# A four-layer vision network on one core: who goes first while the last image is sampled, and which engine makes the feed-forward's casts after the scan

## The chip, the cores and the metric

The kernel runs on one core of one Trainium2 chip. The core has a matrix engine (TensorE, in the profile PE, with PEld for its weight loads), a vector engine (VectorE, DVE), a scalar engine (ScalarE, ACT), a general engine (GpSimd, POOL) and a queue for transfers (SyncE, SP). Each engine works through its own list of instructions in order; semaphores tie the lists together. The metric is the time of one execution on the device, in microseconds (us), lower is better.

## The reference, cut to what matters

Four images of 96 channels and 64x64 pixels pass through four layers, each added to its input:

```python
# layer 0: group norm, depthwise conv, selective scan in four directions, gate, projection
x = x + _L0_conv_ref(_gn(x), ...)
# layer 1: group norm, deformable 3x3 convolution (9 taps, bilinear sampling, mask)
x = x + _L1_conv_ref(_gn(x), ...)
t = _to_tokens(x)                        # 4096 tokens of 96
# layer 2: Fourier mixing, then a feed-forward in quantized arithmetic
t = t + _L2_attn_ref(_ln_t(t), ...)
t = t + _L2_ffn_ref(_ln_t(t), ...)
# layer 3: linear attention, then the same feed-forward with other weights
t = t + _L3_attn_ref(_ln_t(t), ...)
t = t + _L3_ffn_ref(_ln_t(t), ...)
```

The feed-forward (`_qlinear` twice, with a ReLU between) rounds each factor to a float of 5 exponent and 2 mantissa bits and each sum to 5 and 10 bits. In the kernel these are casts to an fp8 and an fp16 type: 96 to 384 to 96 values per token.

## The kernel before, in words

**Three kinds of work, two streams and a scan.** Layer 0's selective scan (`Layer0.scan`) is one long loop of 1536 units; it sets the pace of the program until about 7904 us. Everything else is written as generators that hand out small steps: an instruction or a few, with a cost for each engine that the planner books. Two streams of such steps exist (`layers23`, at the end of the file). `ends()` is stream 0: it prepares layer 0's inputs and then takes image 0, 1, 2 and 3 through layers 2 and 3 (`Layers23.image`), one after the other. `middle()` is stream 1: for each image it finishes layer 0 (`Layer0.behind`) and does layer 1 (`Layer1.image`). An image may enter layers 2 and 3 only when its layer 1 is through (`while b not in self.net.sampled`), and only when the image before it has left.

**The planner.** `Clock` keeps, at build time, an end of planned work for each engine. A step is issued if the engines that it needs are not booked too far ahead (`AHEAD`) and its inputs are planned to be ready; otherwise the stream is passed over. `go()` asks both streams for a step, in a fixed order: `reversed(streams)`, so stream 1 has the first choice. What is issued is recorded, and `in_program_order` fixes that order on each engine. `pipe` does the same inside a stream, among the chains of one stage. The order of the instructions is thus settled when the program is built; the chip only follows it. The scan's `goes` steps take part until it ends; then the scan's PSUM banks are given back, `net.own_banks` is set (five banks for stream 0, three for stream 1), and `alone()` runs the two streams until both are over.

**Sampling an image** (`Layer1.sample`, helper `taps`). An image has 32 blocks of 128 pixels with 9 taps each, taken three at a time: 96 triples. For a triple GpSimd issues three indirect transfers (L1301), each fetching for 128 pixels the four corners of a tap from a table in DRAM; they land in a buffer `g`, of which there are six. VectorE multiplies by the four weights (L1310). Once `own_banks` is set, VectorE also adds the corners (L1314, L1315), so that TensorE needs 3 transposes (L1327) instead of 12; ScalarE copies them to `st` (L1335), which frees `g`. After six triples TensorE applies the convolution's weights (L1343), VectorE adds bias and input (L1348), and SyncE stores the piece (L1350).

**Layers 2 and 3 of an image.** SyncE loads the image, `t` (L1679). `Fourier.run` normalises, multiplies by DFT matrices (L1421 the 64x64 ones) and adds to `t` (L1508). `Ffn.run` normalises into `tl` (L1525, in `normed`; the trace calls it `fl`) and works in 8 chunks of 512 tokens, up to four at once: a cast to `xq` (L1567; two buffers), three matmuls (L1572) with copies to `h16` (L1573; two buffers), bias and ReLU in three pieces (on VectorE, L1578, once `own_banks` is set, else on ScalarE, L1582), a cast to `h8` (L1585; two buffers), three matmuls (L1589), a copy to `o16` (L1591; two buffers), the bias (L1594 or L1596) and the residual add (L1598). Both casts are GpSimd's:

```python
nc.gpsimd.tensor_copy(xq, tl[:, cs], saturate=False)      # L1567
nc.gpsimd.tensor_copy(h8, h16, saturate=False)            # L1585
```

`LinearAttention.run` comes between the two feed-forwards; it begins with a memset on GpSimd (L1618) and ends with adds to `t` (L1654). At the end SyncE stores `t` (L1686).

Of the kernel before, what the change touches and what calls it, by code (L numbers as in the profile page):

```python
# [19 lines left out]
B, C, H, W = 4, 96, 64, 64  # L20
# [152 lines left out]
class Step:  # L173
# [5 lines left out]
    def __init__(self, work, wait=0.0, holds=0, new=False, takes="", frees=""):  # L179
        self.work, self.wait, self.holds, self.new = work, wait, holds, new  # L180
        self.takes, self.frees = takes.split(), frees.split()


def cost(pe=0.0, dve=0.0, act=0.0, pool=0.0, **more):
    return Step((pe, dve, act, pool), **more)


def wait(us=0.0, **more):

    return Step((0.0,) * 4, us, **more)  # L190
# [155 lines left out]
class Net:  # L346
# [3 lines left out]
    def __init__(self, ctx, tc, ins):  # L350
        self.tc, self.nc, self.ins = tc, tc.nc, ins
        nc = self.nc
        self.const = ctx.enter_context(tc.tile_pool(name="const", bufs=1))
        self.dram = ctx.enter_context(tc.tile_pool(name="scratch", bufs=1, space=DRAM))
        self.psum = ctx.enter_context(tc.tile_pool(name="mm", bufs=3, space=PSUM))
        for name in ("vecs", "ident", "cen96", "grp3", "add4"):
            setattr(self, name, self.load(name, self.const))

        self.to_row = {}
        for n in (C, DI):  # L360
            t = self.to_row[n] = self.const.tile([128, 65], F32, name=f"to_row{n}")
            nc.vector.memset(t, 0.0)
            nc.vector.memset(t[:, 1:2], 1.0 / n)
        self.eps = self.const.tile([128, 1], F32, name="eps")
        nc.vector.memset(self.eps, 1e-5)
        self.one = self.const.tile([128, 1], F32, name="one")
        nc.vector.memset(self.one, 1.0)
        self.minus_one = self.const.tile([128, 1], F32, name="minus_one")
        nc.vector.memset(self.minus_one, -1.0)
        self.exp_and_log()  # L370

        self.sampled = set()
        self.clock, self.known, self.streams, self.stream = Clock(), {}, [], None

        self.own_banks = None
# [740 lines left out]
class Layer1:  # L1116
# [23 lines left out]
    def image(self, b):  # L1140
        tc = self.net.tc
        with tc.tile_pool(name=f"l1i{b}", bufs=1, side="right") as ix:
            idx = ix.tile([128, 288], U32, name=f"idx{b}", tag="idx")
            wt = ix.tile([128, 288, 4], F32, name=f"wt{b}", tag="wt")
            yield from self.before(b, idx, wt)
            yield from self.sample(b, idx, wt)
        self.net.sampled.add(b)

# [208 lines left out]
class Fourier:  # L1357
# [77 lines left out]
    def run(self, b, t):  # L1435

        net = self.net
        tc, nc = net.tc, net.nc
        with tc.tile_pool(name=f"l2b{b}", bufs=1) as big:
            tl = big.tile([C + 1, L], F32, name=f"tl{b}", tag="tl")  # L1440
            nc.gpsimd.memset(tl[C:], 1.0)
            with tc.tile_pool(name=f"l2n{b}", bufs=2) as pool:
                yield from normed(net, t, tl, f"2_{b}", pool)
            tv = tl.rearrange("c (n1 n2) -> c n1 n2", n2=64)
            with tc.tile_pool(name=f"l2s{b}", bufs=2) as pool:
                for g in range(2):
                    yield from self.half(f"{b}_{g}", g, tv, t, pool, pool)
# [83 lines left out]
class Ffn:  # L1531
# [23 lines left out]
    def run(self, b, t):  # L1555
        net, n = self.net, self.n
        tc, nc = net.tc, net.nc
        with tc.tile_pool(name=f"fb{n}_{b}", bufs=1) as big, tc.tile_pool(name=f"fs{n}_{b}", bufs=2) as pool:
            tl = big.tile([C, L], F32, name=f"fl{n}_{b}", tag="tl")
            yield from normed(net, t, tl, f"f{n}_{b}", pool)  # L1560

            def chunk(j):
                yield wait(takes="xq")
                cs = slice(j * CH, (j + 1) * CH)
                key = f"f{n}_{b}_{j}"
                xq = pool.tile([C, CH], F8, name=f"xq{key}", tag="xq")
                nc.gpsimd.tensor_copy(xq, tl[:, cs], saturate=False)  # L1567
                yield cost(pool=0.8, new=True, takes="h16")
                h16 = pool.tile([128, 3, CH], F16, name=f"h16{key}", tag="h16")
                for g in range(3):  # L1570
                    ph = net.mm(f"ph{key}_{g}")
                    nc.tensor.matmul(ph, lhsT=self.w1[:, 128 * g : 128 * g + 128], rhs=xq, start=True, stop=True)  # L1572
                    nc.scalar.copy(h16[:, g], ph)  # L1573
                yield cost(pe=1.3, act=1.8, frees="xq")
                if net.own_banks:
                    for g in range(3):
                        bias = self.bias[:, g : g + 1]
                        nc.vector.tensor_scalar(h16[:, g], h16[:, g], bias, 0.0, ALU.add, ALU.max)  # L1578
                    yield cost(dve=1.5, takes="h8")
                else:  # L1580
                    for g in range(3):
                        nc.scalar.activation(h16[:, g], h16[:, g], AF.Relu, bias=self.bias[:, g : g + 1])  # L1582
                    yield cost(act=2.1, takes="h8")
                h8 = pool.tile([128, 3, CH], F8, name=f"h8{key}", tag="h8")
                nc.gpsimd.tensor_copy(h8, h16, saturate=False)  # L1585
                yield cost(pool=1.5, new=True, takes="o16", frees="h16")
                po = net.mm(f"po{key}")
                for g in range(3):
                    nc.tensor.matmul(po, lhsT=self.w2[:, g, :], rhs=h8[:, g], start=(g == 0), stop=(g == 2))  # L1589
                o16 = pool.tile([C, CH], F16, name=f"o16{key}", tag="o16")  # L1590
                nc.scalar.copy(o16, po[:C])  # L1591
                if net.own_banks:
                    yield cost(pe=1.3, act=0.6, frees="h8")
                    nc.vector.tensor_scalar_add(o16, o16, self.bias[:C, 3:4])  # L1594
                else:
                    nc.scalar.activation(o16, o16, AF.Identity, bias=self.bias[:C, 3:4])  # L1596
                    yield cost(pe=1.3, act=1.3, frees="h8")
                nc.vector.tensor_add(t[:, cs], t[:, cs], o16)  # L1598
                yield cost(dve=1.0, frees="o16")

            yield from pipe(self.net, (chunk(j) for j in range(NCH)), 4, xq=2, h16=2, h8=2, o16=2)


# [93 lines left out]
def layers23(net, x2, out):  # L1697

    with ExitStack() as ctx:
        l0 = Layer0(ctx, net, net.x1)
        l1 = Layer1(ctx, net, net.x1, x2)

        def ends():
            yield from l0.before(0)
            l23 = Layers23(ctx, net, x2, out)
            yield from l23.prepare()
            yield from l0.before(1)  # L1710
            yield from l0.before(2)
            yield from l0.before(3)
            for b in range(B):
                yield from l23.image(b)

        def middle():
            yield from l1.cleared()
            for b in range(B):
                yield from l0.behind(b)
                yield from l1.image(b)  # L1720

        streams = net.streams = [Stream(net, ends()), Stream(net, middle())]
        clock = net.clock

        def go():

            return any([stream.step() for stream in reversed(streams)])

        def alone():

            if clock.own is None:
                clock.own = max(clock.ends)
            if not go():
                clock.own += 0.5

        for goes in l0.scan():
            if not goes:
                alone()
                continue
            if clock.own is not None:  # L1740
                clock.due = max(clock.due, clock.own + PACE)
                clock.idle = max(clock.idle, clock.due)
                clock.own = None
            while go():
                pass
        l0.banks.close()
        net.own_banks = ctx.enter_context(net.tc.tile_pool(name="own", bufs=5, space=PSUM))
        while not all(stream.over for stream in streams):
            alone()
        net.in_program_order()  # L1750
# [24 lines left out]
```

## Time and profile before

| what | value |
|---|---|
| median of 4 runs | 9101.74 us (9082.23 to 9113.54) |
| the profiled execution's own time | 9094.06 us |
| its span, first to last instruction | 9092.3 us |
| busy over the span | PE 72%, DVE 77%, POOL 70%, ACT 46% |
| last unit of the scan | 7904 us |
| image 3 sampled (L1310) | 8080 to 8532 us |
| image 2 in layers 2 and 3 (L1679 to L1686) | 7563 to 8626 us |
| image 3 in layers 2 and 3 | 8633 to 9084 us |

The page of the profile gives shares over the whole span, and most of the span is the scan. For a change that begins after the scan one has to ask for stretches: busy time in a window, groups of instructions in a window, and the order of single instructions on one engine. In a row of a group, "x96" is the count, then follow busy time, mean duration in ns of one, the engine's idle time just before these instructions, and what ended most of it. A releaser "issue" means that the engine waited for nothing that the profile shows.

### The profile page before, as it was taken

The numbers are of one execution on the slowest core, as the hardware profiler recorded it, in microseconds if no ns is written. First come the engines' busy times: TensorE is split into PE (matmuls) and PEld (weight loads), VectorE is DVE, ScalarE is ACT, GpSimd is POOL, SyncE is SP. The second block draws the span as 40 slices with busy tenths as digits, with TensorE's granted clock in tenths as the row PEclk, the third lists the DMA queues.
The fourth block names the chain that finished last, engine by engine and source line by source line (L and its number), as shares of the span: only waits on it lengthen the run. The fifth ranks groups of instructions, "written<-read, shape, count | busy, mean of one in ns | idle before, by whom it ended". The sixth has DMA issues, their size and how long they took to land.

```text
span 9092.3 us, 93188 instructions
## 1 busy us (share of the span) xinstructions
PE 6577.2 (72%) x31951; PEld 2981.8 (33%) x31960; DVE 6972.6 (77%) x4932; ACT 4183.6 (46%) x5798; POOL 6382.7 (70%) x4755
## 2 busy tenths in 40 slices
PE   6664977697766668777667777777777677874687
PEld 2111311132222234211224554223554332462374
DVE  0367878887788889888789898988999998636514
ACT  4564667565544435556443334554333444321223
POOL 0486679766788989788799895775898966538501
PEclk8675977798777779877778888878888887886788
DMA  1466787777777788787778878677888776644210
GB/s 51 125 185 167 189 203 223 195 192 191 192 209 207 205 205 221 194 211 208 201 205 203 224 205 193 171 172 188 214 212 213 190 176 171 156 129 138 76 54 12
DMA packets 775967, 1608.21 MB, mean 177 GB/s; under 512 B 247809, under 2 KB 339357, under 8 KB 773382
## 3 DMA queue, kind: packets, MB, share of 16 engines
q10 hardware_dynamic: 244224, 843.17, 37.0%
q1 hardware_dynamic: 457542, 532.51, 21.9%
q0 software_dynamic: 73728, 226.57, 9.4%
q8 instruction: 255, 4.18, 0.2%
q14 instruction: 218, 1.79, 0.1%
HBM read 1345.62 MB, written 256.29 MB: 176 GB/s over the span
## 4 chain that ended last, share of the span: by engine, by line
PE 33%; DVE 20%; DMA 15%; POOL 13%; issue 10%; ACT 6%; SPq 2%; ACTq 1%; another core or an unknown queue 0%; DVEq 0%; POOLq 0%
DVE hh L961 9%; POOL hh L970 6%; DVE db L953 5%; PE pc L692 5%; PE py L989 3%; PE ps L1327 3%; PE f L1421 3%; DMA du<-du 3%; PE db L939 3%; POOL g L1301 2%; PE pd L1343 2%; DVE g L1310 1%; DMA da<-de 1%; DMA m<-in_dft 1%; POOL lw L781 1%
## 5 line engine op out<-in xcount | busy, mean ns | idle before, releaser
L970 POOL TENSOR_TENSOR hh<-hh,bc 128x1024 f32<-128x1024 f32 x1536 | 3655.8, 2383 | 347.4 <-DVE hh L961 235.6
L961 DVE TENSOR_TENSOR_SCAN hh<-da,st,db 128x1024 f32<-128x1024 f32 x1152 | 2700.7, 2344 | 176.9 <-PE py L989 50.3
L953 DVE TENSOR_TENSOR db<-db,bc 128x1024 f32<-128x1024 f32 x1536 | 1864.5, 1214 | 510.9 <-PE db L939 495.2
L933 ACT ACTIVATE da<-da,w_al 128x1024 f32<-128x1024 f32 x1536 | 1740.1, 1147 | 847.7 <-DMA da<-de 395.3
L939 PE MATMUL db<-du,rep 96*128 96x512 bf16 x3072 | 1088.8, 443 | 816.5 <-DVE hh L961 725.1
L1301 POOL DMA_INDIRECT g<-table,idx x1152 | 1339.1, 1162 | 369.9 <-issue 233.9
L989 PE MATMUL py<-hh,w_fold 128*32 128x512 f32 x6144 | 1075.7, 741 | 87.2 <-POOL hh L970 64.3
L1327 PE MATMUL ps<-w_ident,g 128*96 128x128 f32 x3744 | 637.6, 333 | 517.1 <-issue 294.6
L961 DVE TENSOR_TENSOR_SCAN hh<-da,db 128x1024 f32<-128x1024 f32 x384 | 876.7, 2283 | 55.8 <-PE py L989 19.8
L939 PEld LDWEIGHTS <-rep 96*128 96x128 bf16 x3072 | 278.9, 106 | 1781.9 <-issue 1135.9
L1310 DVE TENSOR_TENSOR g<-g,wt 128x1152 f32<-128x1152 f32 x384 | 724.6, 1889 | 107.2 <-DMA g<-table,idx 96.9
L1327 PEld LDWEIGHTS ps<-w_ident,g 128*96 128x96 f32 x3744 | 517.9, 155 | 792.3 <-issue 417.4
L1335 ACT COPY st<-ps 96x384 f32<-96x384 f32 x384 | 181.9, 476 | 1256.7 <-PE ps L1327 954.8
L968 POOL COPY st<-hh 128x1 f32<-128x1 f32 x1152 | 303.6, 264 | 509.9 <-DVE hh L961 457.8
L780 POOL TENSOR_TENSOR w<-w,ex 128x512 f32<-128x512 f32 x192 | 245.2, 1277 | 496.4 <-ACT w L777 495.3
L692 PE MATMUL pc<-pad,wc 96*128 96x512 f32 x1152 | 545.0, 613 | 47.0 <-DMA wc<-wc_d 43.9
L783 DVE SCALAR_TENSOR_TENSOR rl<-pd,lw 128x512 f32<-128x512 f32 x192 | 131.3, 684 | 417.1 <-POOL lw L781 401.3
L802 PE MATMUL pr<-ex,w_ident 128*128 128x512 f32 x384 | 290.1, 847 | 149.5 <-POOL ex L786 64.3
L1567 POOL CAST xqf<-fl 96x512 fp8e5<-96x512 f32 x64 | 44.9, 710 | 498.1 <-DVE fl L1525 459.2
L989 PEld LDWEIGHTS py<-hh,w_fold 128*32 128x32 f32 x6144 | 159.5, 121 | 598.9 <-issue 375.3
L692 PEld LDWEIGHTS pc<-pad,wc 96*128 96x128 f32 x1152 | 218.0, 195 | 319.3 <-issue 299.2
L770 PE MATMUL pd<-xd,w_dtw 103*64 103x512 f32 (+1 forms) x512 | 273.5, 813 | 65.1 <-DMA w_dtw<-in_dtw 29.5
(249 smaller groups left out, 9198.1 us busy)
## 6 DMA issues: line engine op xcount, KB each, us to landing
da<-de ACTq DMA_DIRECT2D x1536, 512.0 KB
du<-du SPq DMA_DIRECT2D x512, 192.0 KB
bc<-bcd SPq DMA_DIRECT2D x128, 512.0 KB
du<-du SPq DMA_DIRECT2D x128, 384.0 KB
y<-yb SPq DMA_DIRECT2D x384, 128.0 KB
de<-rl SPq DMA_DIRECT2D x128, 256.0 KB
m<-in_dft SPq DMA_DIRECT2D x128, 256.0 KB
ad<-y ACTq DMA_DIRECT2D x192, 128.0 KB
```

The source lines that it names most:

```text
L692: nc.tensor.matmul(pp, lhsT=wc[:, q, g * 128 : (g + 1) * 128], rhs=pad[:, r0 + dy : r0 + dy + NR, dx : dx + W], start=(q == 0), stop=(q == 8),
L802: nc.tensor.matmul(pr, lhsT=net.ident, rhs=ex, start=True, stop=False)
L933: self.net.nc.scalar.activation(u.da, u.da, AF.Exp, scale=self.al[:, a : a + 1])
L939: self.net.nc.tensor.matmul(db[:, h, :], lhsT=self.rep[:96, u.s % 4, :], rhs=u.du[u.s // 4][:, h * CH : (h + 1) * CH], start=True, stop=True,)
L953: self.net.nc.vector.tensor_mul(u.db, u.db, u.bc[:, 0, :])
L961: nc.vector.tensor_tensor_scan(u.along(u.hh), u.along(u.da), u.along(u.db), first, ALU.mult, ALU.add)
L968: self.net.nc.gpsimd.tensor_copy(u.state[:, u.n : u.n + 1], u.hh[:, last : last + 1])
L970: self.net.nc.gpsimd.tensor_mul(u.hh, u.hh, u.bc[:, 1, :])
L989: nc.tensor.matmul(py[p0 : p0 + 32], lhsT=self.fold[:, u.i, :], rhs=hc[:, h * CH : (h + 1) * CH], start=u.sums["add"] is None and u.i == 0 ...
L1301: nc.gpsimd.indirect_dma_start(out=g[:, k, :], out_offset=None, in_=self.tables[b % 2], in_offset=bass.IndirectOffsetOnAxis(ap=idx[:, n : ...
L1310: nc.vector.tensor_mul(g4, g4, w4.unsqueeze(2).to_broadcast([128, 12, C]))
L1327: nc.tensor.matmul(pt[:, k, :], lhsT=g[:, k, c * C : (c + 1) * C], rhs=net.ident, is_transpose=True, start=(c == 0), stop=(c == corners - 1),)
```

## The change

While image 3, the last one, is being sampled, the order in which the planner asks the streams is turned round: stream 0 (layers 2 and 3, at that time of image 2) is asked first. And in the feed-forward, once the scan is over and `own_banks` is set, both casts are VectorE's instead of GpSimd's; the costs booked for them change with that. While the scan runs, nothing changes.

```diff
 class Net:
         self.sampled = set()
+        self.sampling_last = False
...
 class Layer1, image():
             yield from self.before(b, idx, wt)
+            self.net.sampling_last = b == B - 1
             yield from self.sample(b, idx, wt)
...
 class Ffn, run():
-                nc.gpsimd.tensor_copy(xq, tl[:, cs], saturate=False)
-                yield cost(pool=0.8, new=True, takes="h16")
+                if net.own_banks:
+                    nc.vector.tensor_copy(xq, tl[:, cs], saturate=False)
+                    yield cost(dve=0.4, new=True, takes="h16")
+                else:
+                    nc.gpsimd.tensor_copy(xq, tl[:, cs], saturate=False)
+                    yield cost(pool=0.8, new=True, takes="h16")
...
-                nc.gpsimd.tensor_copy(h8, h16, saturate=False)
-                yield cost(pool=1.5, new=True, takes="o16", frees="h16")
+                if net.own_banks:
+                    nc.vector.tensor_copy(h8, h16, saturate=False)
+                    yield cost(dve=1.0, new=True, takes="o16", frees="h16")
+                else:
+                    nc.gpsimd.tensor_copy(h8, h16, saturate=False)
+                    yield cost(pool=1.5, new=True, takes="o16", frees="h16")
...
 layers23(), go():
-            return any([stream.step() for stream in reversed(streams)])
+            return any([stream.step() for stream in (streams if net.sampling_last else streams[::-1])])
```

The flag is set when the sampling of image 3 is about to begin and stays set to the end of the program; from then on the feed-forwards of image 2 and of image 3 (32 chunks in all) are still to come.

## The prediction

> **What bounds the kernel now.** All times are microseconds from the start of the span. I first placed the change in time. In the two built programs the instruction queues are the same, engine by engine, up to the first sampled taps of image 3, so nothing before 8073 can move. Then I read busy time by stretch, because shares over the whole span say nothing about the last tenth of it. The columns are the stretch, its length, then busy time (and instructions) of PE, PEld, DVE, ACT and POOL, the granted clock, DMA share and GB/s.
>
> ```profile
> 8073.00:8104.00 31.00, 21.19 (x240) 17.99 (x238) 15.45 (x18) 4.00 (x7) 20.35 (x18) 0.67 0.46 133
> 8104.00:8200.00 96.00, 63.62 (x356) 48.23 (x356) 59.28 (x69) 16.64 (x35) 75.35 (x63) 0.77 0.52 154
> 8200.00:8362.00 162.00, 76.80 (x269) 48.98 (x268) 104.12 (x129) 27.74 (x57) 128.18 (x112) 0.67 0.49 144
> 8362.00:8460.00 98.00, 44.70 (x153) 26.35 (x152) 73.55 (x98) 24.61 (x49) 83.51 (x70) 0.60 0.40 116
> 8460.00:8538.00 78.00, 46.41 (x157) 27.07 (x157) 49.11 (x62) 18.04 (x37) 52.57 (x44) 0.71 0.40 114
> 8538.00:8633.00 95.00, 68.67 (x241) 32.68 (x240) 42.07 (x61) 37.10 (x85) 21.31 (x17) 0.83 0.06 18
> ```
>
> Image 3 is sampled from 8073 to 8538. From 8538 to 8633 only what is left of image 2 in layers 2 and 3 runs. Next, SyncE's issues in order of time (start, length, line, transfer):
>
> ```profile
> 8538.03 0.30 SPq L1350 DMA_DIRECT2D x<-xo  x1
> 8625.64 0.32 SPq L1686 DMA_DIRECT2D out<-t  x1
> 8632.91 0.30 SPq L1679 DMA_DIRECT2D t<-x  x1
> ```
>
> The last sampled piece of image 3 is stored at 8538.0, but image 3 enters layer 2 (L1679) only at 8632.9, when image 2 has left (its output store goes at 8625.6). That is 94.9 us in which the sampled image waits. From 8632.9 to the end of the span, 9092.3, are 459.4 us of image 3 alone. What bounds the sampling is in GpSimd's groups from 8073 to 8530 (busy, mean ns, idle before and its releasers):
>
> ```profile
> L1301 POOL DMA_INDIRECT g<-table,idx x288 | 339.8, 1180 | 162.9 <-DVE wt L1281 71.3 <-issue 69.9 <-PE ps L1327 6.9
> L1585 POOL CAST h8f<-h16f 128x1536 fp8e5<-128x1536 f16 x8 | 11.8, 1478 | 0.0
> L1567 POOL CAST xqf<-fl 96x512 fp8e5<-96x512 f32 x8 | 4.9, 624 | 0.0
> L1618 POOL MEMSET tl<- 1x4096 f32 x1 | 3.5, 3506 | 0.0
> ```
>
> 339.8 + (162.9 − 71.3) + 11.8 + 4.9 + 3.5 = 451.6: first gather 8073.4, last one done at 8525.1, no gap but 0.3 us of issue after each gather and 6.9 us of waiting for PE. The sampling is GpSimd's queue, end to end. Each three gathers ("a triple", 96 of them) fill one of six g buffers.
>
> VectorE in the same stretch, for the prices:
>
> ```profile
> L1310 DVE TENSOR_TENSOR g<-g,wt 128x1152 f32<-128x1152 f32 x96 | 129.9, 1353 | 90.2 <-DMA g<-table,idx 80.2 <-issue 10.0
> L1314 DVE TENSOR_TENSOR g<-g 128x576 f32<-128x576 f32 x96 | 72.8, 758 | 3.3
> L1315 DVE TENSOR_TENSOR g<-g 128x288 f32<-128x288 f32 x96 | 52.9, 551 | 3.3
> ```
>
> It waits 80.2 us for gathers: there is room in it.
>
> **The change, part by part.** *Order.* In the changed program VectorE meets the first feed-forward of image 2 between its 18th and 26th triple (62nd to 82nd before), and the last residual add of the second after the 67th, before which the old order had not begun it. So image 2 leaves well before the sampling ends, and the 94.9 us turn into: when does the last gather end? The sum is GpSimd's queue again.
>
> Removed from it: 8 xq and 8 h8 casts, 4.9 + 11.8 = 16.7 us. The memset (L1618) stays; it now stands after triple 32, behind image 2's first feed-forward, whose last work on VectorE stands before triple 27, so I cost its wait at nothing: the gathers of triples 27 to 32 (6 × 4.5 us) cover it, and if that cover is gone it is a wait like those of b.
>
> Added, a: the start. The transposes (L1327) of the first triple now stand on PE behind all 77 remaining DFT matmuls instead of 45, and the fourth triple's product on VectorE behind two residual adds (L1508). Six buffers are full after 26 us; the wait there is 5.9 us today. 32 more matmuls take 2 us at the pace of the stretch where gathers rested (66 in 4.4 us at 8099.7) and up to 13 us at the pace beside gathers (8113.6 to 8126.5). Range 0 to 20, I take 10, the middle, since both paces occur.
>
> b: the two feed-forwards. VectorE has per chunk xq + 3 biases + h8 + o16 bias + residual add. Biases 0.34, o16 0.34, add 0.69 are the undisturbed rows. The casts are not in the trace on VectorE. xq, 512 elements f32: bounds 0.43 (the f32 to bf16 cast of 128x512, L569) and 0.69 (a two-input op of 512); nearest is the cast, 0.43. h8, 1536 elements: L1314 and L1315 (0.76 and, undisturbed, 0.46) give 0.16 us + 1.04 ns per element for two inputs, so at most 1.76; the f16 bias gives (0.34 − 0.16)/512, so at least 0.72; the casts of 576 elements (L1262, 0.46) give 0.97. I take 0.97: also a cast with one side four bytes or one. Sum 0.43 + 1.02 + 0.97 + 0.34 + 0.69 = 3.45 a chunk, 27.6 for eight. With eight triples at 1.35 + 0.76 + 0.46 = 2.57 that is 48 us, 51 with waits, in which GpSimd alone would do 51/4.5 = 11.3 triples. VectorE falls 3.3 triples behind; a triple occupies its buffer some 11 us (2.5 triples), so 3.5 buffers are spare. It just fits: 0 to 30 us for both, I take 10.
>
> c: the gathers themselves. Beside VectorE a gather is longer:
>
> ```profile
> 8377.69 0.69 DVE L1598 TENSOR_TENSOR t<-t,o16f 96x512 f32<-96x512 f32 x1
> 8377.85 2.62 POOL L1301 DMA_INDIRECT g<-table,idx  x1 [0.30 <-issue]
> 8378.31 1.34 DVE L1310 TENSOR_TENSOR g<-g,wt 128x1152 f32<-128x1152 f32 x1
> 8379.68 0.76 DVE L1314 TENSOR_TENSOR g<-g 128x576 f32<-128x576 f32 x1
> 8380.48 1.47 POOL L1585 CAST h8f<-h16f 128x1536 fp8e5<-128x1536 f16 x1
> 8380.48 1.79 DVE L1315 TENSOR_TENSOR g<-g 128x288 f32<-128x288 f32 x1
> ```
>
> 2.62 us instead of 0.95, ending when L1314 ends; and the casts on GpSimd hold VectorE up in turn (L1315 1.79 instead of 0.46). From 8200 to 8360, little else running, 110 gathers average 1.155; from 8405 to 8455, in the feed-forward, 28 average 1.312. If the 201 gathers that now run beside layers take 1.312 and the other 87 take 1.155, it is 364.2, 24 us more. Range 0 to 24, I take 12.
>
> [...]
>
> Last gather: 8073.4 + 451.7 − 16.7 + 10 + 10 + 12 = 8540.4. To image 3's load: landing 2.6, products 2.6, transposes and copy 1.4, the last nine matmuls 3.9, xo 0.6, together 11.2; and the store's landing, between 0 and 7.1 (the sixteen times larger out store, 8625.6 to 8632.7): 2.5. So 8554 instead of 8632.9: −79.
>
> *Casts of image 3, alone.* Today its feed-forward takes 27.0 us after the last normalising product (9057.1 to 9084.1), with VectorE slowed by GpSimd's casts: eight residual adds average 1426 ns. Now all is on VectorE: 27.6, and the order puts four chunks in a group, in which the first o16 bias waits about 1 us for ScalarE ahead of the third h8: 29.6. Twice +2.6 = +5. Bounds −1.8 (h8 0.72, no wait) to +11 (h8 1.76, xq 0.69) each.
>
> Sum: −79 + 5 = −74. The profiled execution took 9094.06, 7.7 below the median of the runs shown; against the median the forecast is 9101.74 − 74 = **9028**. Low end, all terms at their best: 451.7 − 16.7, no landing, −3.6: −117, 8985. High end 20 + 30 + 24, landing 7.1, +22: −10, 9091.
>
> **Rivals.** *The feed-forward holds the gathers.* For it: beside the sampling the first feed-forward took 8362 to about 8455 before. Against: there the gathers went first. If it now takes 80 us for 8 triples, GpSimd stands for 80 − 36 − 16 = 28 us in each: 9028 − 10 + 56 = 9074.
>
> *VectorE starves the gathers* (slower). Place: the 201 gathers beside layers; price: their mean. 74 + 12 = 86 us are used up at 1.18 + 86/201 = 1.61 us. At 1.89, as the gather at 8371.8 took behind both L1310 and L1314, c is 143 and the time 9028 − 12 + 143 = 9159. Against: the busiest 50 us give 1.312.
>
> *A larger gain:* a, b and c near zero, 8985 to 9005. Against: the 5.9 us wait shows the start is tight already.
>
> **How the numbers follow.** 0.3% is 27 us, about what this measurement can tell from no change. Forecast (9005 to 9055) 0.55; larger gain 0.10; feed-forward holding, 9055 to 9075, 0.13; the same further on or gathers near 1.6 us, within 27 us of before, 0.12; slower 0.10. Faster 0.78. The range 8985 to 9085 leaves out some 0.17.
>
> **What would show it.** Right: L1679 for image 3 right behind the last xo store, near 8554; out of image 2 some 150 us before; GpSimd without casts, gathers at 1.2 to 1.25, waits for PE some 25 us; L1585 on VectorE near 0.97; the part from L1679 to the end near 465. Wrong: a mean gather over 1.6, or waits of GpSimd for PE or VectorE over 60 us.

## The result and the profile after

| what | before | after |
|---|---|---|
| median of the runs | 9092.36 us (56 runs, 9046.49 to 9139.84) | 9041.77 us (35 runs, 9007.18 to 9080.33) |
| ratio to before, 95% interval | | 0.995 (0.9939 to 0.996) |
| span of the profiled execution | 9092.3 us | 9051.8 us |

The changed kernel is faster by half a per cent: some 45 us by the ratio, 51 by the medians; 74 were forecast. The two spans differ by 40.5 us, so the traces hold the difference, and it can be cut up. Lines of the changed file: up to L1527 they are the old ones plus 2 (plus 1 ahead of L1146); behind that L1573 became L1579, L1578 L1584, L1585 L1592 (on VectorE) or L1595, L1598 L1608, L1618 L1628, L1679 L1689 and L1686 L1696.

First the order. SyncE's issues in the changed kernel (start, duration, line, operation, output and input): image 2 leaves 125 us before the sampling ends, and image 3 is loaded 1.8 us after the store of its last piece.

```profile
8462.83 0.42 SPq L1696 DMA_DIRECT2D out<-t  x1
...
8588.21 0.30 SPq L1352 DMA_DIRECT2D x<-xo  x1
8589.99 0.30 SPq L1689 DMA_DIRECT2D t<-x  x1
```

Now GpSimd's queue. The groups of GpSimd in the changed kernel, 8040 to 8600 us (count, busy time, mean ns, idle time before and its releasers), and then its waits in the same stretch (total, times, longest):

```profile
L1303 POOL DMA_INDIRECT g<-table,idx x288 | 332.2, 1153 | 228.5 <-DVE wt L1283 71.5 <-issue 65.4 <-PE ps L1329 50.0
L1628 POOL MEMSET tl<- 1x4096 f32 x1 | 3.5, 3509 | 0.0
```

```profile
POOL g L1303 <- PE ps L1329: 50.0, 20, 16.2
POOL g L1303 <- PE p L1649: 11.0, 1, 11.0
POOL g L1303 <- DVE g L1316: 10.8, 25, 3.5
POOL g L1303 <- remote: 10.4, 4, 4.5
```

No cast is left there, and a gather is shorter than before, 1153 ns against 1180. But GpSimd now stands still for 228.5 − 71.5 (before the first gather) − 65.4 (issue) = 91.6 us; before it was 162.9 − 71.3 − 69.9 = 21.7. (Some 0.3 us stand behind any gather, and where the trace names a releaser they count as waiting: about 22 of the 91.6 and 16 of the 21.7.) The six buffers `g` that are filled in turn are called the ring below, and a wait for one of them to come free a hold. Gathers −7.6, casts −16.7, issue −4.5, waits +69.9: first to last gather became 492.7 us instead of 451.7. The balance of the two traces:

| stretch | before | after | difference | forecast |
|---|---|---|---|---|
| first gather to end of the last | 451.7 | 492.7 | +41.0 | +15.3 |
| end of the last gather to image 3's load | 107.8 | 24.4 | −83.4 | −94.2 |
| that load to the end | 459.4 | 461.8 | +2.4 | +5 |

With the first gather 0.5 earlier, that is −40.5.

The waits stand mainly in five places. At the opening, between 8074 and 8155, GpSimd's row has 36 gathers in the changed kernel, whose first one began just ahead of that, and 52 in the one before. The changed kernel:

```profile
L1303 POOL DMA_INDIRECT g<-table,idx x36 | 41.2, 1143 | 39.9 <-PE ps L1329 26.6 <-issue 9.1 <-DVE g L1316 4.1
```

The kernel before (71.3 of its idle time lie ahead of the first gather):

```profile
L1301 POOL DMA_INDIRECT g<-table,idx x52 | 60.9, 1172 | 93.3 <-DVE wt L1281 71.3 <-issue 13.7 <-PE ps L1327 5.9
```

Beside image 2's first feed-forward (8196 to 8247) GpSimd's row has 27 gathers at 1316 ns and 9.4 us of waiting beyond issue (the second: 26 at 1364 ns, 5.7 us). Between them lie 11.0 us in which the transposes queue behind the attention's matmuls (L1649), and ahead of the last two xo are 3.1 and 4.5 us.

The casts on VectorE, from the last feed-forward of image 3, 9012 to 9044, where nothing runs beside it:

```profile
L1592 DVE CAST h8f<-h16f 128x1536 fp8e5<-128x1536 f16 x8 | 7.7, 957 | 0.3
L1584 DVE TENSOR_SCALAR h16f<-h16f,bias 128x512 f16<-128x512 f16 x24 | 7.0, 346 | 0.0
L1608 DVE TENSOR_TENSOR t<-t,o16f 96x512 f32<-96x512 f32 x8 | 5.5, 688 | 0.3
L1570 DVE CAST xqf<-fl 96x512 fp8e5<-96x512 f32 x8 | 3.2, 419 | 2.0 <-PE phf L1578 2.0
L1604 DVE TENSOR_SCALAR o16f<-o16f,bias 96x512 f16<-96x512 f16 x8 | 2.8, 346 | 3.9 <-ACT o16f L1601 3.9
```

The prices are those of the forecast (0.97 and 0.43). The waits, 2.0 and 3.9 us, are not.

### The profile page after: what moved, and what is told of

Read it like the earlier page. It is cut to its first block, busy times and chain, and to the rows that moved or that the text cites. A ratio compares the mean times of both kernels' runs of the same rounds, so it can differ in the third digit from the quotient of the medians.

```text
span 9051.8 us, 93154 instructions
## 1 busy us (share of the span) xinstructions
PE 6619.0 (73%) x31951; PEld 2997.9 (33%) x31960; DVE 6951.8 (77%) x4996; ACT 4187.3 (46%) x5798; POOL 6302.1 (70%) x4691
## 4 chain that ended last, share of the span: by engine, by line
PE 32%; DVE 20%; DMA 16%; POOL 13%; issue 10%; ACT 6%; SPq 1%; ACTq 1%; another core or an unknown queue 0%; DVEq 0%; POOLq 0%
DVE hh L962 9%; POOL hh L971 6%; DVE db L954 6%; PE pc L693 4%; PE py L990 3%; PE ps L1329 3%; PE db L940 3%; PE f L1423 3%; DMA du<-du 3%; POOL g L1303 3%; DMA da<-de 2%; PE pd L1345 2%; DVE g L1312 2%; DMA m<-in_dft 2%; POOL lw L782 1%
## 5 line engine op out<-in xcount | busy, mean ns | idle before, releaser
L771 PE MATMUL pd<-xd,w_dtw 103*64 103x512 f32 (+1 forms) x512 | 276.5, 815 | 66.6 <-DMA w_dtw<-in_dtw 30.7
L1345 PE MATMUL pd<-st,wdc 96*128 96x256 f32 x1152 | 312.3, 424 | 11.4 <-ACT st L1337 11.4
```

The source lines that it names most:

```text
L1345: nc.tensor.matmul(po, lhsT=wdc[:, k, :], rhs=st[:, k, :], start=(k == 0), stop=(k == 8))
```

## The experiments

The questions: does the order make the gain, or the casts? Is GpSimd's queue really paid instruction by instruction? What are the new waits, and can they be had back? All ratios are to the kernel before, with 95% intervals. Kernels 1 to 4, 5 to 8 and 9 to 12 shared a chip, on which the kernel before took 9080.69, 9079.97 and 9082.80 us. The times in the expectations are for a kernel before at 9092.36, so they are compared by the ratio: 0.9944, for instance, is 9041 there.

**1. The order alone.**

```diff
-                if net.own_banks:
+                if False:
                     nc.vector.tensor_copy(xq, tl[:, cs], saturate=False)
...
-                if net.own_banks:
+                if False:
                     nc.vector.tensor_copy(h8, h16, saturate=False)
```

> The order is turned as in the changed kernel, but all casts of the feed-forwards stay on GpSimd. Theory Q (GpSimd's queue with its waits sets the end of image 3's sampling, so that every instruction put into it is paid): both feed-forwards of image 2 now stand in the queue ahead of the last gather, 32 casts of 0.62 and 1.48 us, 33 us more than in the changed kernel, and GpSimd also waits at their head for h16 and fl; image 3 alone gets back 9 us (VectorE without casts). 9041.8 + 33 - 9 = 9066, up to 9095 with the waits at the head. Rival R (the turned order alone made the gain, the casts were hidden in GpSimd's idle time): 9042 - 9 = 9033 or a little less.

Measured: 9041.63 us, ratio 0.9946 (0.9922 to 0.997). Neither the 9066 of theory Q nor quite the 9033 of R: with all casts back on GpSimd the gain is that of the whole change. GpSimd's groups, 8030 to 8600:

```profile
L1303 POOL DMA_INDIRECT g<-table,idx x288 | 336.9, 1170 | 184.7 <-DVE wt L1283 71.5 <-issue 70.1 <-PE ps L1329 29.4
L1595 POOL CAST h8f<-h16f 128x1536 fp8e5<-128x1536 f16 x16 | 24.9, 1574 | 1.7 <-PE phf L1578 1.3 <-DVE h16f L1584 0.3
L1573 POOL CAST xqf<-fl 96x512 fp8e5<-96x512 f32 x16 | 11.6, 745 | 0.1
```

36.5 us of casts are in the queue, and first to last gather takes 491.6 us, against 492.7 with the casts moved: the waits are 184.7 − 71.5 − 70.1 = 43.1 instead of 91.6. So the queue is not simply paid to the last cast: where a cast left, a wait came. (How much of this pair is the granted clock is told below.)

**2. The casts alone.**

```diff
-            self.net.sampling_last = b == B - 1
```

> The casts are VectorE's as in the changed kernel, the sampling keeps the first choice. Theory Q: the load of image 3 (L1679 before) waits again for image 2, whose second feed-forward is left over when the sampling ends; the sampling's end comes 17 us earlier and image 2 follows it in part, each of the three feed-forwards that run alone costs some 5 us more: between 9085 and 9105, no gain worth the name over 9092.4. Rival R2 (the casts alone made the gain): 9042.

Measured: 9082.59 us, ratio 0.9998 (0.998 to 1.0017). Theory Q's range (9085 to 9105) was for a kernel before at 9092.4; here that stood at 9080.69, so "no gain" is what came. First to last gather is 439.6 us, 12 less than before, and worth nothing, because image 3 waits for image 2 again (SyncE's issues):

```profile
8531.87 0.30 SPq L1351 DMA_DIRECT2D x<-xo  x1
8628.84 0.32 SPq L1695 DMA_DIRECT2D out<-t  x1
8636.12 0.30 SPq L1688 DMA_DIRECT2D t<-x  x1
```

**3. The turn at block 8.**

```diff
-            self.net.sampling_last = b == B - 1
...
             def taps(t, k0):
+                if b == B - 1 and t == 8:
+                    net.sampling_last = True
                 yield wait(takes="g")
```

> As the changed kernel, but the order is turned only at block 8 of the 32 of image 3's sampling (24 of its 96 triples). Theory Q: the opening waits of GpSimd (32.6 us in the changed kernel's trace between 8078 and 8160, the first transposes queued behind all matmuls of a DFT) go back to some 6 us, and image 2, which had left 127 us before the sampling ended, still leaves before it: 9041.8 - 26 = 9016, bounds 9010 to 9030. Rival M (the waits only move, since the layers' matmuls have to run some time beside the gathers): 9037 to 9047.

Measured: 9026.86 us, ratio 0.9944 (0.9922 to 0.9965). That does not tell it from the changed kernel; it is 9041 where theory Q said 9016 and rival M 9037 to 9047. In the trace both theories have a part: the first wait is 5.9 us instead of 16.2, and a new one stands in the attention's stretch, where there were 11 before:

```profile
8342.78 1.51 POOL L1304 DMA_INDIRECT g<-table,idx  x1 [0.30 <-issue]
8366.53 0.94 POOL L1304 DMA_INDIRECT g<-table,idx  x1 [22.24 <-PE ps L1330]
```

First to last gather is 478.2 us, 14.5 less than with the turn at block 0; image 2 leaves at 8491, still ahead of the last gather at 8535.

**4. The residual of the sampling loaded early.** In the changed kernel VectorE idles before several of the last xo, which the trace puts down to something remote, with five finished triples queued behind. The suspicion was the load of xr.

```diff
                     sts[j] = gp.tile([C, 9, 256], F32, name=f"st{b}_{j}", tag="st")
+                    xrs[j] = gp.tile([C, 256], F32, name=f"xr1_{b}_{j}", tag="xr", bufs=2)
+                    nc.sync.dma_start(xrs[j], self.x1[b][:, cs])
...
-                xr = gp.tile([C, 256], F32, name=f"xr1_{b}_{j}", tag="xr")
-                nc.sync.dma_start(xr, self.x1[b][:, cs])
+                xr = xrs[j]
```

> As the changed kernel, but the residual of each pair of blocks (xr) has two buffers and its load is issued nine matmuls and six triples earlier, at the pair's first triple instead of its last. Theory X (the 17.6 and 9.8 us that VectorE idles before xo at 8541 and 8567, released by something remote, are the landing of that load, 24 us after its issue beside the gathers): GpSimd's last two waits (3.1 and 4.5 us) go, and the last triples follow the last gather at once instead of standing behind xo: image 3's load some 18 us earlier, 9024, bounds 9020 to 9032. Rival I (VectorE waits there for its own instructions or for PE): 9042, and the idle time before xo stays.

Measured: 9011.75 us, ratio 0.9921 (0.9899 to 0.9944); last gather to image 3's load 14.0 us instead of 24.4. By the ratio that is 9021, as theory X had it, though the interval touches the changed kernel's (0.9939 to 0.996); its mechanism did not hold. In the changed kernel the load before the xo at 8567.0 was issued at 8542.3, and the transfers of 8542 to 8546 already hold all its packets, those of 8546 to 8566 none on that queue (queue: packets, MB, share of 16 engines; the first of the two):

```profile
q1 hardware_dynamic: 224, 0.20, 16.7%
```

And idle time until something remote stays before the xo of the kernel with the early load: 22.6 us in all, where the changed kernel has 35.9. What it is the trace shows only in outline. In the changed kernel three engines resume within 0.4 us of each other, 10 us after the last recorded depthwise matmul began (VectorE, ScalarE and GpSimd rows):

```profile
8541.44 0.48 DVE L1350 SCALAR_TENSOR_TENSOR xo<-pd,w_vecs,xr 96x256 f32<-96x256 f32 x1 [17.55 <-remote]
```

```profile
8541.59 0.47 ACT L1337 COPY st<-ps 96x384 f32<-96x384 f32 x1 [13.12 <-remote]
```

```profile
8541.77 2.23 POOL L1303 DMA_INDIRECT g<-table,idx  x1 [4.53 <-remote]
```

All three wait for work of PE (the depthwise product, its release of `st`, a transpose). That PE's end came later than modelled is a reading, not shown. Nor is it shown that the early load shortens the end: from the last gather to image 3's load, experiments 1 and 5, which load xr late, took 15.0 and 14.2 us, and experiment 10, which loads it early, 20.5. The shorter end here may have been the execution's; where the gain in time comes from stays open.

**5. A seventh g buffer.**

```diff
+            ring = 7 if b == B - 1 else 6          # wdc 96 columns wide for image 3
...
-                g = gp.tile([128, 3, 4 * C], F32, name=f"g{key}", tag="g", bufs=6)
+                g = gp.tile([128, 3, 4 * C], F32, name=f"g{key}", tag="g", bufs=ring)
...
-            yield from pipe(self.net, chains, 8, g=6, st=1, xo=1)
+            yield from pipe(self.net, chains, ring + 2, g=ring, st=1, xo=1)
```

> As the changed kernel, with seven g buffers instead of six for image 3 (room for the seventh comes from its depthwise weights, 96 columns wide instead of 128, of which the rows beyond 96 were never read). Theory b2 (GpSimd's 92 us of waits in the changed kernel are a full ring: a triple's product or its transposes stand behind layers' work on VectorE or PE for longer than the spare buffers last): each hold begins one triple, 4.5 us, later, and there are some five to seven of them (opening, both feed-forwards, the chain of the attention, the last xo): first to last gather 492.7 - 20 to 30 = 463 to 473, the time 9042 - 25 = 9017. Rival C (VectorE lacks throughput there, so a buffer only fills once): first to last gather 488 to 493, the time within 5 us of 9042.

Measured: 9023.66 us, ratio 0.9943 (0.9925 to 0.996), which does not tell it from the changed kernel's 0.995. First to last gather 472.9 us looks like theory b2, but the opening wait (16.9 us) and the attention's (11.4) are as long as with six; of the 19.8 us some 12 lie in the second part of the opening, and those go with the granted clock, below. So a buffer more does not shorten the long holds, and theory b2's 25 us fell.

**6 and 7. Late turn and early xr together; image 2's casts on VectorE (6) or on GpSimd (7).** Image 3's casts are on GpSimd in both.

```diff
-                if net.own_banks:
+                if net.own_banks and b < B - 1:     # 6; in 7: if False
```

> The late turn (block 8) and the early xr together, the casts of image 2 on VectorE, those of image 3 on GpSimd. From the single runs: first to last gather 478, 14 to image 3's load instead of 24, the rest 457 as with casts on GpSimd: 34 us less than the changed kernel, 9008; bounds 9000 to 9025. With the next kernel it tells what image 2's casts are worth on VectorE once the opening and the end are better: theory Q says 33 us less than there, theory b2 no difference beyond 6 us.

> The late turn and the early xr, with all casts on GpSimd. Theory b2 (in the feed-forwards beside the sampling GpSimd waits anyway, so casts there cost nothing): first to last gather within 6 us of the kernel with image 2's casts on VectorE, the time 9008, bounds 9000 to 9025. Theory Q (GpSimd's queue is paid to the last cast): 33 us more between first and last gather, 9040.

Measured: 9015.11 us, 0.9928 (0.9916 to 0.994), and 9035.95 us, 0.9962 (0.9944 to 0.9981). The intervals do not touch: for image 2 the casts are better on VectorE, by 21 us in the medians and 31 by the ratios. In the traces first to last gather is 499.1 and 512.1 us, 13 apart. Theory b2 falls; of the 33 us that Q would have paid, between 13 and 31 are, depending on which of these measures is taken. Neither kernel reaches the sum of its parts (478 us was expected): the 22 us hold at the attention is there in both, and the early load did nothing for it.

**8. Only the small cast on VectorE.** As the changed kernel, with the second `if net.own_banks` of experiment 1 set to `if False`.

> As the changed kernel, but only the small cast (xq) is VectorE's, the large one (h8) stays on GpSimd. In the feed-forwards that run alone VectorE then has 2.5 us a chunk instead of 3.45 and no cast that waits ahead of the o16 biases: the last residual add 27 to 29 us after the last product, as in the kernel before, if VectorE's work is the bound (34.5 and 31.2 in the changed kernel); 31 or more if its waits for xq's buffer (2.0 us) and the order are. First to last gather 485 to 495 by theory b2, 485 + 25 = 510 by theory Q. The time 9042 - 6 = 9036, within 0.3% of the changed kernel in any case.

Measured: 9029.71 us, ratio 0.995 (0.9933 to 0.9967): no difference, as expected in any case. The feed-forwards that run alone took 30.9 and 28.6 us from last product to last add: between the changed kernel (34.5, 31.2) and before (29.2, 27.0). VectorE's waits in the last one are down to 0.8 and 0.6 us, but GpSimd's h8 slows its adds (1278 ns a residual add, 688 without). First to last gather 508.3 us is theory Q's number, not b2's, though the kernel of experiment 1 has more casts in that queue and took 491.6: these are single traces, and how far they can be compared is told below.

**9. The early xr on the kernel before.**

> The kernel before with the early load of xr alone. Theory O (in the kernel before, image 3 waits for image 2's leftover work and not for the sampling, so a shorter end of the sampling buys nothing): within 0.2% of the kernel before, and L1679's load still right behind image 2's out. Rival L (every shorter sampling is passed on, since image 2's layers follow it): 0.3% faster, as the same edit gave on top of the turned order (0.9921 against 0.995).

Measured: 9069.65 us, ratio 0.999 (0.9976 to 1.0003). Theory O: image 2 leaves at 8591.6, the load comes at 8598.8, 98 us after the last xo's store. Theory O is not really put to the test by this, since the early load shortened nothing in the trace: first to last gather is 451.7 us as before, and the last xo's store follows 13 us behind, as before. Experiment 2 tests it: its sampling was 12 us shorter, and the time was the same with the order not turned.

**10 to 12. What can be had: turn at block 0 (10) or 3 (11), seven buffers (12).** All have the early xr, image 2's casts on VectorE and image 3's on GpSimd; 12 turns at block 0 and writes the sum into xr to make room.

```diff
-                if b == B - 1 and t == 8:
+                if b == B - 1 and t == 3:           # 11, against 6
```

> The changed kernel with the early xr, and the casts of image 3 alone back on GpSimd. Image 3's feed-forwards then take 29.2 and 27.0 us from last product to last add instead of 34.5 and 31.2, of which some 4 us reach the end (457.4 instead of 461.8 from load to end with all casts on GpSimd); the end of the sampling as with early xr alone. Ratio to before 0.9921 - 0.0005 to 0.001 = 0.9915, some 31 us faster than the changed kernel's 0.995. If image 3's casts were hidden after all: 0.9921.

> As the one before (early xr, image 3's casts on GpSimd), the order turned at block 3 of 32 instead of block 0. Theory a (the 16 us opening wait is the first transposes' place behind all matmuls of one DFT): the wait falls to 6 to 9 us, ratio 0.9905. Rival M (layers' chains hold the ring wherever they fall: with the turn at block 8 a wait of 22 us stood at the attention's chain instead): no gain, 0.9915 to 0.993.

> As the kernel before last (early xr, image 3's casts on GpSimd, turn at block 0), with seven g buffers for image 3; room comes from the narrow depthwise weights and from writing the sum into xr. Theory b2 (a full ring at each hold): three to five holds begin one triple, 4.5 us, later: 13 to 22 us, ratio 0.9895 to 0.990. If the holds are throughput (seven buffers alone gave 0.9943 against 0.995): 0.991.

| kernel | turn | time, us | ratio (95% interval) | first to last gather |
|---|---|---|---|---|
| 10 | block 0 | 9006.89 | 0.9923 (0.9899 to 0.9947) | 485.9 |
| 11 | block 3 | 8980.86 | 0.9893 (0.987 to 0.9917) | 459.8 |
| 6 | block 8 | 9015.11 | 0.9928 (0.9916 to 0.994) | 499.1 |
| 12, seven buffers | block 0 | 8997.65 | 0.9912 (0.9887 to 0.9938) | 477.6 |

Number 11 beats both kernels: 1.1% under before, with an interval clear of the changed kernel's. GpSimd's groups and waits there, 8030 to 8600:

```profile
L1305 POOL DMA_INDIRECT g<-table,idx x288 | 344.0, 1194 | 184.9 <-DVE wt L1282 72.6 <-issue 65.0 <-PE ps L1333 27.6
```

```profile
POOL g L1305 <- PE ps L1333: 27.6, 15, 10.7
...
POOL g L1305 <- remote: 2.3, 1, 2.3
```

184.9 − 72.6 − 65.0 = 47.3 us of waits, half of the changed kernel's; the opening wait is 10.7, with another 7.2 later in the opening, and the holds at the attention and before the last xo are gone. A shorter first wait was expected (6 to 9), the others' going not: the later turn moves every later step of the two streams against each other. Which of these moves took the holds away was not tried. Against number 10, the same kernel turned at block 0, the medians differ by 26 us, but the two intervals overlap a little. Image 3's casts back on GpSimd (10 against experiment 4, 0.9923 and 0.9921) made no difference that can be measured, though its feed-forwards take 29.2 and 27.0 us again. Between 10 and 12 the intervals overlap; a seventh buffer is not shown to be worth anything.

**The granted clock in the traces.** Experiment 1 and the changed kernel have the same order of instructions until image 2's first cast, yet behind the first wait the opening has one more, of 2.9 us, there and three here, of 3.6, 3.5 and 6.8 us, together 13.9. Windows of 25 us, each begun 46 us behind the first gather (window, length, busy time of PE, PEld, DVE, ACT and POOL with counts, then the granted clock, DMA share and GB/s), for the changed kernel, for the order alone and for seven buffers:

```profile
8119.00:8144.00 25.00, 23.38 (x88) 16.31 (x89) 15.31 (x17) 4.81 (x9) 15.21 (x12) 0.50 0.41 121
```

```profile
8085.00:8110.00 25.00, 22.94 (x146) 17.01 (x146) 21.34 (x23) 5.65 (x12) 18.88 (x12) 0.93 0.45 135
```

```profile
8109.00:8134.00 25.00, 21.39 (x155) 16.02 (x154) 20.83 (x22) 5.74 (x11) 19.36 (x15) 1.00 0.52 157
```

At 0.50 PE gets 88 instructions done in the window, at 0.93 and 1.00 146 and 155, and the ring waits for PE. With seven buffers one wait of 1.7 us follows there. Of the seven traces with the turn at block 0, five have the clock at 0.50 for 20 to 38 us at this place, the changed kernel's and those of experiments 4, 8, 10 and 12, and all five have waits of 10 us or more behind the first one (17.6 in experiment 12); the two others, 1 and 5, have neither. The low clock is thus the usual one here; what decides it is not shown. So some 11 to 16 us of a single trace's sampling go with the clock in that execution, and image 3 alone, load to end, took between 436 and 463 us in the traces, the shortest ones at the highest clock (0.86 and 0.92 in its first 150 and next 130 us in the changed kernel, 0.93 and 1.00 in experiment 7, the one at 436). Corrected for that in the pair of experiment 1, the moved casts shorten the sampling by some 10 us (491.6 less 492.7 − 11.0), an estimate from two traces, in line with the 13 of experiments 6 and 7.

## Why the prediction was right or wrong

**The order: right.** "So image 2 leaves well before the sampling ends, and the 94.9 us turn into: when does the last gather end?" Image 2 left at 8463 (150 us ahead of image 3's load was said, 127 came), L1689 follows the last store by 1.8 us (2.5 said), and 1 and 2 show that the order is the whole gain: 0.9946 without the casts, 0.9998 without the order. Rivals "larger gain" and "slower" did not come.

**a, the opening, 10: too small.** GpSimd waited 30.7 us there against 5.9, so a was 25, beyond the range's 20. The named mechanism is the first part, the wait behind the DFT's matmuls: 16.2 us here, 10.3 more than before, which is the 10 that the forecast took. It is 12.6 to 16.9 in the traces with the turn at block 0, 10.7 at block 3, and 5.9 to 9.5 at block 8. That the size came out is in part luck. The 66 that the forecast read as matmuls are records, and a DFT matmul has two of them (the first transposes stand behind 64 records more, not 32), so its 2 us at the fast pace should have been 4.3. The other part, some 14, is a queue behind PE at a granted clock of 0.50, with 2.9 and 1.7 us at 0.93 and 1.00: a term that the forecast did not have.

**b, the feed-forwards, 10: right in size, incomplete in place.** They hold the gathers 9.4 and 5.7 us. But the forecast looked for holds in the feed-forwards alone: 11.0 us at the attention's chain and 7.6 (3.1 and 4.5) before the last xo are waits of the same ring that no term covered. So "waits of GpSimd for PE or VectorE over 60 us", which was to show the forecast wrong, came true (91.6, or some 70 without the 0.3 us behind each gather), and the time was still 0.5% better, because the order's 83 us were larger. "It just fits" was the step that failed: the ring's spare was worked out for one steady mixture, and the long waits are single chains standing ahead in PE's or VectorE's queue, which a seventh buffer did not shorten.

**−16.7 for the casts: right as an item, wrong as a gain.** They left the queue and a gather beside the feed-forward costs what was said (1.316 and 1.364 us, forecast 1.312). But part of the 33 us that two feed-forwards' casts take on GpSimd came back as waits, since VectorE then does both the casts and the triples' products: it is busy 45 of the 51 us of the first feed-forward. The move is worth nothing in the times of experiment 1 against the changed kernel (some 10 us in their traces, corrected for the clock), and 13 to 31 in experiments 6 and 7. This is the rival "the feed-forward holds the gathers", at a third and a fifth of its price (28 us in each).

**c, longer gathers, 12: wrong sign.** All 288 took 7.6 us less. The rate was right beside the feed-forwards, but it was applied to 201 gathers, where 53 are beside one; and the 72 gathers that run after image 2 has left take less:

```profile
L1303 POOL DMA_INDIRECT g<-table,idx x72 | 74.7, 1038 | 31.7 <-issue 16.8 <-remote 7.9 <-DVE t L1608 3.1
```

Single gathers are held all the same. The forecast's gather of 2.62 us (0.95 undisturbed) stood beside products with two inputs, not casts; but beside the moved casts gathers are held too:

```profile
8204.12 1.52 POOL L1303 DMA_INDIRECT g<-table,idx  x1 [0.30 <-issue]
8204.56 0.96 DVE L1592 CAST h8f<-h16f 128x1536 fp8e5<-128x1536 f16 x1
```

This gather ends 0.12 us after the cast, as do five more of the eight in whose course, 0.3 to 0.6 us from their start, an h8 cast begins (the other two end later still, 0.8 and 2.1 us behind it). The 27 gathers that overlap a cast average 1.47 us, the 58 beside no work of VectorE 0.95. Taken as an estimate, that is 27 × 0.52 = 14 us for casts and what runs with them. The total hides it, because the gathers behind image 2 got shorter.

**Last gather to load, 13.6: it took 24.4.** The last triples were not ready behind the last gather: five stood on VectorE behind an xo that idled 9.8 us until something remote. Not foreseen and not fully explained; where no such stall stood at the end it was 14 to 15 (15.0 and 14.2 in experiments 1 and 5, 14.0 in 4).

**Image 3 alone, +5: the feed-forwards cost 9.5.** 34.5 and 31.2 us against 29.2 and 27.0. The prices of the casts were right, and 27.6 us of work too; the step that failed is "the first o16 bias waits about 1 us": VectorE waits 3.9 us for ScalarE's o16 and 2.0 for the buffer of xq. Of this 2.4 us are left in the stretch from load to end, within what the clock moves there. The memset's wait was hidden, as costed. (The lower bound of −1.8 comes to 27.6 − 8 × 0.25 − 27.0 = −1.4 by the forecast's own numbers; nothing hangs on it.)

**Sum.** Terms of the forecast, and what the trace gave: casts −16.7 and −16.7, waits (a and b) +20 and +69.9, gathers and their issue +12 and −12.1, end of sampling −94.2 and −83.4, image 3 +5 and +2.4. The mechanism was right; the waits were mis-sized by 50 us, partly hidden by an error of 24 the other way in c. That the time lies only 14 us above the forecast is also owed to the kernel before, whose median came down from 9101.74 us in 4 runs to 9092.36 in 56: the gain itself was 51 instead of 74.

## What to carry to other kernels

Turning a fixed order round pays what waited at its end, here 83 us, and costs at every place where a long chain of the newly preferred stream now stands ahead of the other's short steps in an in-order queue: look for those chains (a DFT's matmuls, 16.2 us of waiting here; an attention's serial products, 11.0), one by one, rather than for average throughput. Once the order is right, when it turns can matter too: block 3 instead of block 0 brought the waits from 87 to 47 us and the median down by 26, with intervals that still overlap, while block 8 alone gained nothing. An instruction taken out of the queue that bounds a stage is worth its length only if the engine that gets it has room in the same place (VectorE, which got the casts, was busy 45 of the 51 us there); and a single trace can differ by 10 to 25 us with its clock (here 11 to 16 us of the sampling, and 436 to 463 us for image 3 alone), so small edits are judged by repeated times beside those of the kernel before, not by one trace.

## What was not expected of the hardware

The granted clock can stay at 0.50 for 25 us while PE is busy for 94% of them (23.38 us, 8119 to 8144 in the changed kernel), in a place where experiments 1 and 5 had 0.93 and 1.00; 11 us more of waits in another engine's queue go with it. Where a large cast began on VectorE 0.3 to 0.6 us into a gather of GpSimd, the gather ended 0.12 us behind that cast in six of eight cases, so a cast taken off GpSimd can still lengthen what GpSimd does. And several engines can stand still for 6 to 10 us behind a depthwise product whose last matmul is recorded as begun, until something that the trace calls remote; it happened in the changed kernel three times in the last 130 us of the sampling, and not once in the trace of the kernel before, nor in that of experiment 11. VectorE's xo in the changed kernel, 8380 to 8600, and in experiment 11:

```profile
L1350 DVE SCALAR_TENSOR_TENSOR xo<-pd,w_vecs,xr 96x256 f32<-96x256 f32 x8 | 3.8, 478 | 50.6 <-remote 35.9 <-PE pd L1345 8.7 <-PE ps L1329 5.9
```

```profile
L1353 DVE SCALAR_TENSOR_TENSOR xo<-pd,w_vecs,xr 96x256 f32<-96x256 f32 x6 | 2.9, 479 | 13.8 <-PE pd L1348 11.7 <-issue 2.1
```
